# A transformer block with routed experts: the third pair of routed tiles turned from its first rows, and another order of work at the start

## The chip, the cores and the metric

The kernel runs on one core of a Trainium2 chip. The core has five engines that run their own instruction streams: TensorE (PE) multiplies matrices, with a separate record for loading weights (PEld), VectorE (DVE) does elementwise work and small transposes, ScalarE (ACT) activations and copies, GpSimd (POOL) elementwise work and the indirect DMAs, and SyncE (SP) issues most of the other DMAs. The metric is the device time of one execution in microseconds (us); lower is better.

## What is computed

The input is x of 16 sequences, 512 tokens each, 256 numbers a token, all in float32. With xn the layer norm of x over its 256 numbers, the result is

```
out = x + attention(xn) + ffn(xn)

attention:  q = elu(xn Wq + bq) + 1,  k = elu(xn Wk + bk) + 1,  v = xn Wv + bv     (16 heads of 16)
            kv = sum over tokens of k v^T, per head
            out = (q kv) / max(q . sum of k, 1e-6), then Wo and bo

ffn:        shared = swiglu(xn w_in) w_out                                        (hidden 512)
            h = swiglu(xn w1)                                                     (hidden 512)
            one of 2 groups by the larger group logit; in it the best 2 of 4 experts by softmax,
            weighted by their probability times that of the group
            routed = sum over the two experts of weight_e * (h w2_e)
```

## The kernel before, in words

**Sequence by sequence.** The 16 sequences are worked one after another, each as four token tiles of 128. `normalize` (line 249) makes xn on VectorE (bn_stats L263, bn_aggr L265, reciprocal L268, subtract and multiply L270; the square root is ScalarE's, L267) and brings it into the transposed form xnT. For the first two sequences TensorE transposes (L280) and ScalarE copies to SBUF (L283); from the third on xn goes to DRAM, comes back in blocks of 32 rows (`turn`, L232, xb), and one VectorE instruction transposes the blocks (L242). `project` (L304) makes keys and router logits in one product (pk, L312) and queries (pq, L323); VectorE adds the biases (kk L316, lg L317, qq L327) and `feature_map` (L297) applies elu + 1. `route` (L333) computes groups, experts and weights in many small VectorE instructions. `residual` (L289) has POOL add bo to x (L292). These run a sequence ahead as `front` (L725).

**The rest of a sequence.** `summarize` (L464) multiplies xn with the keys, `hidden_rows` (L417) makes h row by row and stores it to a DRAM table h_d (L433), `hidden` (L435) makes the shared hidden part, `mix` (L477) combines the key summary with Wv and Wo, and `gather` (L526) adds shared output and attention for each token tile in PSUM (po, L534, two buffers); VectorE adds it to the residual (L535), and the base row is stored to the same table h_d (L536), behind h.

**The routed tiles.** After the last sequence the tokens are sorted by their pair of experts (`order`, L539). The class `Tiles` (L642) takes two tiles of 128 sorted tokens at a time, 33 such pairs and one single tile. `rows` (L649) fetches their rows of h_d by indirect DMA on POOL's queue, one of each tile (L654), into one of four row buffers which are the old kk, qq, xn and hs. `turn` (L660) transposes h: ScalarE makes 12 copies of quarters (hb, L673) and VectorE 4 + 3 block transposes (L680 straight from the rows, L686 from the copies) into hT, which has two buffers. `sums` (L692) multiplies hT with the two experts' weights side by side (py, L703), VectorE weights both and adds the base (y, L710 and L713), and an indirect DMA on POOL scatters y to the output (L716). With `AHEAD = 3`, the first three pairs are fetched once before the last `gather`, when h is complete but the base isn't, and again after it. Only the first two are turned from the first fetch (L775, L776).

**What sets the order.** [...] `tc.issue_after(ins)` places what is traced inside it behind `ins` on its engine; `tc.keep_in_program_order` keeps an instruction in the program's order. A buffer of a pool is reused when the last reader of its old tile is done. PSUM has six buffers for most products (`ps_mm`) and two for po. At the start, x comes in four pieces on SP's queue, wk and wq on ScalarE's, and the small weights we and wg and the biases on POOL's.

Of the kernel before, what the change touches and what calls it, by code (L numbers as in the profile page):

```python
# [10 lines left out]
FP = mybir.dt.float32  # L11
AF = mybir.ActivationFunctionType
ALU = mybir.AluOpType
AX = mybir.AxisListType

P = 128
# [5 lines left out]
def block_kernel(  # L22
# [29 lines left out]
    nc = tc.nc  # L52
    B, S, D = x.shape
# [7 lines left out]
    NT = S // P  # L61
# [15 lines left out]
    AHEAD = 3  # L77
# [12 lines left out]
    ps_mm = ctx.enter_context(tc.tile_pool(name="ps_mm", bufs=6, space=bass.MemoryType.PSUM))  # L90
# [28 lines left out]
    nc.gpsimd.memset(eps_sb, LN_EPS)  # L119
    ident = const.tile([P, P], FP)  # L120
    make_identity(nc, ident)
    root = const.tile([P, 1], FP)
    nc.scalar.activation(root, eps_sb, AF.Sqrt)

# [5 lines left out]
    nc.gpsimd.dma_start(out=wkr_sb[:, :, D : D + E], in_=we.rearrange("(p c) e -> p c e", p=P))  # L130
    nc.gpsimd.dma_start(out=wkr_sb[:, :, D + E : KR], in_=wg.rearrange("(p c) e -> p c e", p=P))
    wq_sb = wp.tile([P, KD, D], FP)
    nc.scalar.dma_start(out=wq_sb, in_=wq.rearrange("(p c) f -> p c f", p=P))
    bkr_sb = const.tile([P, KR], FP)
    nc.gpsimd.dma_start(out=bkr_sb[:, 0:D], in_=bk.partition_broadcast(P))
    nc.gpsimd.dma_start(out=bkr_sb[:, D : D + E], in_=eb.partition_broadcast(P))
# [4 lines left out]
    for q in range(NQ):  # L141
        nc.gpsimd.dma_start(
            out=bv_sb[ts(q, Q)], in_=bv[ts(q, KD * Q)].rearrange("(c i) -> i c", i=Q)
# [10 lines left out]
    for k in range(KD):  # L154
        for c in range(KD):
            nc.sync.dma_start(
                out=wv_sb[:, k, ts(c, P)].rearrange("p (q i) -> p q i", i=Q), in_=by_quadrant(wv[ts(k, P), :])[:, c]
            )
    wo_sb = wp.tile([P, KD, D], FP)
    for q in range(NQ):  # L160
        nc.sync.dma_start(
            out=wo_sb[ts(q, Q)], in_=wo[ts(q, KD * Q), :].rearrange("(c i) d -> i c d", i=Q)
# [5 lines left out]
    def load_expert(i):  # L168
# [23 lines left out]
        out=before, in_=ones, pattern=[[1, P]],  # L192
# [56 lines left out]
    def normalize(b):  # L249

        xt = xs[b]
        st = small.tile([P, NT, 6], FP, tag="st", name=f"st_{b}")
        mv = small.tile([P, NT, 2], FP, tag="mv", name=f"mv_{b}")
        sd = small.tile([P, NT], FP, tag="sd", name=f"sd_{b}")
        rs = small.tile([P, NT], FP, tag="rs", name=f"rs_{b}")
        xn = xn_all[:, b % 2]

        n = 1 if b == 0 else NT
        made = []
        for g in range(0, NT, n):  # L260
            with tc.issue_after(last_xn[-1].ins) if last_xn else nullcontext():
                for t in range(g, g + n):
                    nc.vector.bn_stats(out=st[:, t, :], in_=xt[:, t, :])  # L263
            for t in range(g, g + n):
                nc.vector.bn_aggr(out=mv[:, t, :], in_=st[:, t, :])  # L265
            with tc.issue_after(last_copy[-1].ins) if last_copy else nullcontext():
                nc.scalar.activation(sd[:, g : g + n], mv[:, g : g + n, 1], AF.Sqrt, bias=eps_sb)  # L267
            nc.vector.reciprocal(rs[:, g : g + n], sd[:, g : g + n])  # L268
            for t in range(g, g + n):
                made.append(nc.vector.tensor_scalar(  # L270
                    xn[:, t, :], xt[:, t, :], mv[:, t, 0:1], rs[:, t : t + 1],
                    ALU.subtract, ALU.mult,
                ))
        last_xn[:] = made[-1:]
        xnT = work.tile([P, KD, S], FP, tag="xnT", name=f"xnT_{b}")
        if b < 2:
            for t in range(NT):
                pt = ps_mm.tile([P, KD, P], FP, tag="mm", name=f"pt_{b}_{t}")
                for c in range(KD):
                    nc.tensor.transpose(  # L280
                        pt[:, c, :], xn[:, t, :].rearrange("p (m c) -> p c m", c=KD)[:, c], ident
                    )
                last_copy.append(nc.scalar.copy(xnT[:, :, ts(t, P)], pt))  # L283
            return xn, xnT, None
        last_copy.clear()
        nc.sync.dma_start(out=xn_d[b % 2].rearrange("(t p) d -> p t d", p=P), in_=xn)
        return xn, xnT, turn(xnT, xn_d[b % 2], "xb", b, "(i c)")
# [13 lines left out]
        nc.scalar.activation(low, low, AF.Exp)  # L301
        nc.vector.scalar_tensor_tensor(y, y, 0.0, low, ALU.max, ALU.add)

    def project(b, xnT):  # L304

        kk = kk_all[:, b % 2]
        qq = qq_all[:, b % 2]
        lg = small.tile([P, NT, E + G], FP, tag="lg", name=f"lg_{b}")
        for t in range(NT):
            pk = ps_mm.tile([P, KR], FP, tag="mm", name=f"pk_{b}_{t}")  # L310
            for k in range(KD):
                nc.tensor.matmul(  # L312
                    pk, lhsT=xnT[:, k, ts(t, P)], rhs=wkr_sb[:, k, :],
                    start=(k == 0), stop=(k == KD - 1),
                )
            nc.vector.tensor_tensor(kk[:, t, :], pk[:, 0:D], bkr_sb[:, 0:D], ALU.add)  # L316
            nc.vector.tensor_tensor(lg[:, t, :], pk[:, D:KR], bkr_sb[:, D:KR], ALU.add)  # L317
        feature_map(b, kk, "km")
        for t2 in range(0, NT, 2):
            pq = ps_mm.tile([P, 2, D], FP, tag="mm", name=f"pq_{b}_{t2}")  # L320
            for t in (0, 1):
                for k in range(KD):
                    nc.tensor.matmul(  # L323
                        pq[:, t, :], lhsT=xnT[:, k, ts(t2 + t, P)], rhs=wq_sb[:, k, :],
                        start=(k == 0), stop=(k == KD - 1),
                    )
            nc.vector.tensor_tensor(  # L327
                qq[:, t2 : t2 + 2, :], pq, bq_sb.unsqueeze(1).to_broadcast([P, 2, D]), ALU.add
            )
        feature_map(b, qq, "qm")  # L330
        return qq, kk, lg
# [191 lines left out]
        qT = one.tile([P, KD, S], FP, tag="qT", name=f"qT_{b}")  # L523
        return qT, turn(qT, q_d[b % 2], "qb", b, "(c i)")

    def gather(b, res, qT, kvo, hs):  # L526

        taken = []
        for t in range(NT):
            po = ps_y.tile([P, D], FP, tag="py", name=f"po_{b}_{t}")  # L530
            parts = [(hs[:, f, ts(t, P)], wout_sb[:, f, :]) for f in range(KH)]
            parts += [(qT[:, c, ts(t, P)], kvo[:, c, :]) for c in range(KD)]
            for i, (a, w) in enumerate(parts):
                nc.tensor.matmul(po, lhsT=a, rhs=w, start=(i == 0), stop=(i == len(parts) - 1))  # L534
            taken.append(nc.vector.tensor_tensor(res[:, t, 0:D], po, res[:, t, 0:D], ALU.add))  # L535
            nc.sync.dma_start(out=h_d[ts(b * NT + t, P), HID:ROW], in_=res[:, t, :])  # L536
        return taken

# [103 lines left out]
    class Tiles:  # L642
# [17 lines left out]
        def turn(self, after=None):  # L660

            n, W = self.n, HID // NQ
            self.hT = work.tile([P, KH, 2 * P], FP, tag="xnT", name=f"hT_{self.tiles[0]}")
            to = self.hT.rearrange("p c (n a j) -> p n c a j", n=2, a=NQ)[:, 0:n]
            near = 1
            there = work.tile([P, NQ - near, 2, W], FP, tag="blocks", name=f"hb_{self.tiles[0]}")  # L670
            for a in range(near, NQ):
                for q in range(NQ):
                    nc.scalar.copy(  # L673
                        there[ts(q, Q), a - near, 0:n, :], self.hg[ts(a, Q), 0:n, ts(q, W)]
                    )
            wait = (lambda: tc.issue_after(after.ins)) if after else nullcontext
            for a in range(near):
                for q in range(NQ):
                    with wait():
                        nc.vector.transpose(  # L680
                            to[ts(q, Q), :, :, a, :],
                            self.hg[ts(a, Q), 0:n, ts(q, W)].rearrange("p n (c i) -> p n c i", i=Q),
                        )
            for a in range(near, NQ):
                with wait():
                    nc.vector.transpose(  # L686
                        to[:, :, :, a, :],
                        there[:, a - near, 0:n, :].rearrange("p n (c i) -> p n c i", i=Q),
                    )
            return self  # L690

        def sums(self):  # L692

            for j, i in enumerate(self.tiles):
                if i % TR == 0:
# [6 lines left out]
                for f in range(KH):  # L702
# [4 lines left out]
                    )  # L707
                base = self.hg[:, j, HID:ROW]
                y = work.tile([P, D], FP, tag="y", name=f"y_{i}", bufs=4)
                nc.vector.scalar_tensor_tensor(  # L710
                    y, py[:, 0, :], base[:, D : D + 1], base[:, 0:D], ALU.mult, ALU.add
                )
                nc.vector.scalar_tensor_tensor(  # L713
                    y, py[:, 1, :], base[:, D + 1 : D + 2], y, ALU.mult, ALU.add
                )
# [6 lines left out]
                tc.declare_no_dep(stored.ins, group="out", reason="no two tiles write to the same row")  # L722
                tc.add_to_no_dep_group("out", stored.ins)

    def front(b, xnT):  # L725

        res = residual(b)
        qq, kk, lg = project(b, xnT)
        route(b, lg, res)
        return res, qq, kk  # L730

    waiting = list(range(G * NL))

    normed = {0: normalize(0)}
    fronts = {0: front(0, normed[0][1])}
    normed[1] = normalize(1)
    queries = {}
    xs[2] = load_x(2)
    for b in range(B):
# [24 lines left out]
            queries[b + 1] = attend(b + 1, fronts[b + 1][1], sums)  # L764
        hs = hidden(b, xnT)
        kvo = mix(b, xk, ksb)
        if b + 2 < B:
            normed[b + 2][2]()
        if b + 1 == B:
            for w in tiles[:AHEAD]:  # L770
                w.rows()
        taken = gather(b, res, qT, kvo, hs)
        if b + 1 == B:

            tiles[0].turn(taken[-2])  # L775
            tiles[1].turn(taken[-1])  # L776

        for e in waiting[: 2 if b + 1 < B else G * NL]:
            load_expert(e)
# [9 lines left out]
    for g, w in enumerate(tiles):  # L789
        if 0 < g < len(tiles) - AHEAD:  # L790
            tiles[g + AHEAD].rows()
        if g + AHEAD - 1 < len(tiles):
            tiles[g + AHEAD - 1].turn()
        w.sums()

    def rest(i):
        if i < TILES:
# [44 lines left out]
```

## Time and profile before

| What | us |
|---|---|
| three runs: lowest, median, highest | 1086.5, 1091.64, 1130.06 |
| the profiled execution: its own time | 1087.99 |
| the profiled execution: span from first to last instruction | 1086.2 |
| TensorE busy, of the span | 1055.5 |
| VectorE, ScalarE, POOL busy | 660.9, 375.9, 243.9 |
| first transpose, first pk on TensorE | 8.18, 10.69 |
| first pk of the second sequence, first phr | 20.13, 31.14 |
| first py of the routed tiles | 833.45 |

The profile names an engine, a line and the tiles that an instruction writes and reads ("py<-w_sb,hT"). A float32 product appears as two records for each matmul, so a routed tile (four matmuls) has eight records of py, a pair sixteen. A wait is written with what ended it, for instance "PE py L703 <- DVE hT L686". PEclk is the share of full speed that TensorE's clock was granted. The few times that TensorE waits are at the start, once after the first sequence, and between the last sequence and the routed tiles.

### The profile page before, as it was taken

Reading aid. Unit: us, or ns where it says so; the run is one execution under the profiler, and the core shown is the slowest. Engines: PE = TensorE matmul, PEld = TensorE weight load, DVE = VectorE, ACT = ScalarE, POOL = GpSimd, SP = SyncE. Lnnn points to the kernel's source line nnn. Section 1 sums busy time; section 2 is a strip of 40 time slices with the busy share of each in tenths; the row PEclk is TensorE's granted clock in tenths of the full one; section 3 lists DMA queues with packets and bytes.
Section 4 is the critical chain, followed back from the end, with each engine's and each line's share of the span. In section 5 each row is a group of like instructions: output and inputs, shape, how many; then the busy total and the mean of one; then the engine's idle time right before and its main releaser. Section 6 shows DMA issues by size and latency. Waiting matters only on the chain.

```text
span 1086.2 us, 11307 instructions
## 1 busy us (share of the span) xinstructions
PE 1055.5 (97%) x3404; PEld 627.5 (58%) x3404; DVE 660.9 (61%) x1744; ACT 375.9 (35%) x703; POOL 243.9 (22%) x313
## 2 busy tenths in 40 slices
PE   6999999999999999999999999999999699999996
PEld 5574747575666657574747575666646244444442
DVE  7947466564647474746556464647395466666663
ACT  3413232223223131313222232212013667777761
POOL 6102011020202020101101020202003555555552
PEclk9999999999999999999999999999999899999999
DMA  7243342433424243423131323221114544555540
GB/s 228 97 117 117 78 135 59 135 92 105 133 69 136 69 136 88 125 59 115 41 116 57 100 72 91 81 63 63 59 40 133 185 136 152 150 151 152 153 151 34
DMA packets 129054, 116.02 MB, mean 107 GB/s; under 512 B 72109, under 2 KB 113597, under 8 KB 128736
## 3 DMA queue, kind: packets, MB, share of 16 engines
q1 hardware_dynamic: 119120, 77.16, 23.7%
q0 software_dynamic: 9456, 37.59, 11.4%
q8 instruction: 29, 0.48, 0.2%
q10 hardware_dynamic: 416, 0.52, 0.1%
q14 instruction: 33, 0.27, 0.1%
HBM read 65.36 MB, written 50.27 MB: 106 GB/s over the span
## 4 chain that ended last, share of the span: by engine, by line
PE 94%; DVE 2%; DMA 1%; issue 1%; ACT 0%; POOL 0%; SPq 0%; POOLq 0%; DVEq 0%; ACTq 0%
PE py L703 21%; PE phr L424 20%; PE phs L443 20%; PE po L534 15%; PE pxk L469 5%; PE pk L312 5%; PE pq L323 5%; PE pm L499 2%; PE pvk L482 1%; PE pks L459 1%; DMA x<-in_x 0%; DMA xn_all<-h_d,source 0%; ACT hb L673 0%; DMA hs_all<-h_d,source 0%; PE pi L614 0%
## 5 line engine op out<-in xcount | busy, mean ns | idle before, releaser
L703 PE MATMUL py<-w_sb,hT 128*128 x536 | 233.5, 599 | 10.0 <-DVE hT L686 10.0
L443 PE MATMUL phs<-xnT,win_sb 128*128 128x512 f32 x512 | 223.6, 593 | 0.0
L424 PE MATMUL phr<-w_sb,xnT 128*128 128x512 f32 x512 | 222.8, 593 | 0.0
L703 PEld LDWEIGHTS py<-w_sb,hT 128*128 128x128 f32 x536 | 103.0, 193 | 140.0 <-issue 138.9
L424 PEld LDWEIGHTS phr<-w_sb,xnT 128*128 128x128 f32 x512 | 97.3, 190 | 114.5 <-issue 106.0
L443 PEld LDWEIGHTS phs<-xnT,win_sb 128*128 128x128 f32 x512 | 97.0, 190 | 113.0 <-issue 110.3
L292 POOL TENSOR_TENSOR res<-x,bo_sb 128x1024 f32<-128x1024 f32 x16 | 37.9, 2369 | 433.9 <-DMA h_d<-res 323.4
L534 PE MATMUL po<-wout_sb,hs_all 128*128 128x256 f32 x512 | 123.6, 380 | 0.0
L535 DVE TENSOR_TENSOR res<-po,res 128x256 f32<-128x256 f32 x64 | 27.2, 424 | 131.8 <-PE po L534 131.8
L534 PEld LDWEIGHTS po<-wout_sb,hs_all 128*128 128x128 f32 x512 | 96.3, 191 | 12.2
L450 DVE TENSOR_TENSOR hs_all<-phs,sa_hs 128x512 f32<-128x512 f32 x64 | 43.5, 680 | 90.7 <-PE phs L443 85.4
L449 ACT ACTIVATE sa_hs<-phs 128x512 f32<-128x512 f32 x64 | 38.2, 597 | 158.4 <-PE phs L443 153.3
L716 POOL DMA_INDIRECT out<-y,goal x67 | 67.6, 1009 | 88.4 <-DVE y L713 78.0
L301 ACT ACTIVATE km<-km 128x1024 f32<-128x1024 f32 x16 | 16.9, 1057 | 177.4 <-DVE km L300 177.4
L432 DVE TENSOR_TENSOR hr<-phr,sa_hr 128x512 f32<-128x512 f32 x64 | 43.8, 684 | 55.7 <-PE phr L424 32.8
L430 ACT ACTIVATE sa_hr<-phr 128x512 f32<-128x512 f32 x64 | 38.0, 597 | 99.2 <-PE phr L424 93.3
L534 PE MATMUL po<-kvo,qT 128*128 128x256 f32 x256 | 67.0, 384 | 0.0
L312 PE MATMUL pk<-wkr_sb,xnT 128*128 128x266 f32 x256 | 61.3, 393 | 2.0 <-DVE xnT L242 1.7
L469 PE MATMUL pxk<-kk_all,xn_all 128*128 128x256 f32 x256 | 58.0, 380 | 0.0
L323 PE MATMUL pq<-wq_sb,xnT 128*128 128x256 f32 x256 | 57.9, 379 | 0.0
L456 POOL TENSOR_TENSOR k<-kk_all 128x512 f32<-128x512 f32 x16 | 27.6, 1727 | 127.8 <-DVE sm L358 125.3
L312 PEld LDWEIGHTS pk<-wkr_sb,xnT 128*128 128x128 f32 x256 | 49.1, 193 | 11.3 <-DVE xnT L242 2.1
(148 smaller groups left out, 1261.5 us busy)
## 6 DMA issues: line engine op xcount, KB each, us to landing
h_d<-hr SPq DMA_DIRECT2D x64, 256.0 KB, 2.6
h_d<-res SPq DMA_DIRECT2D x64, 129.0 KB, 1.9
q_d<-qq_all SPq DMA_DIRECT2D x16, 512.0 KB, 2.8
qb<-q_d SPq DMA_DIRECT2D x64, 128.0 KB, 2.6
w_sb<-in_w SPq DMA_DIRECT2D x64, 128.0 KB, 3.5
x<-in_x SPq DMA_DIRECT2D x15, 512.0 KB, 4.3
xn_d<-xn_all SPq DMA_DIRECT2D x14, 512.0 KB, 3.0
xb<-xn_d SPq DMA_DIRECT2D x56, 128.0 KB, 3.3
```

What stands on the lines that cost most here:

```text
L312: nc.tensor.matmul(pk, lhsT=xnT[:, k, ts(t, P)], rhs=wkr_sb[:, k, :], start=(k == 0), stop=(k == KD - 1),)
L323: nc.tensor.matmul(pq[:, t, :], lhsT=xnT[:, k, ts(t2 + t, P)], rhs=wq_sb[:, k, :], start=(k == 0), stop=(k == KD - 1),)
L424: nc.tensor.matmul(ph, lhsT=xnT[:, k, ts(t, P)], rhs=w1_sb[:, k, ts(half, HID)], start=(k == 0), stop=(k == KD - 1),)
L430: nc.scalar.activation(sa, halves[0], AF.Silu)
L432: nc.vector.tensor_tensor(hr, halves[1], sa, ALU.mult)
L443: nc.tensor.matmul(ph, lhsT=win_sb[:, k, ts(half * KH + f, P)], rhs=xnT[:, k, :], start=(k == 0), stop=(k == KD - 1),)
L449: nc.scalar.activation(sa, halves[0], AF.Silu)
L450: nc.vector.tensor_tensor(h[:, f, :], halves[1], sa, ALU.mult)
L469: nc.tensor.matmul(pxk[:, c, :], lhsT=xn[:, t, ts(c, P)], rhs=kk[:, t, :], start=(t == 0), stop=(t == NT - 1),)
L534: nc.tensor.matmul(po, lhsT=a, rhs=w, start=(i == 0), stop=(i == len(parts) - 1))
L703: nc.tensor.matmul(py.rearrange("p j d -> p (j d)"), lhsT=self.hT[:, f, ts(j, P)], rhs=w2_sb[:, f, bass.ds(regs[i % TR], 2 * D)], start=(f ...
L716: stored = nc.gpsimd.indirect_dma_start(out=out_rows, out_offset=bass.IndirectOffsetOnAxis(ap=self.goal[:, i : i + 1], axis=0), in_=y, in_ ...
```

## The change

The change has three parts.

At the start, TensorE makes eight transposes of the identity into two PSUM tiles that nobody reads, ahead of its first work. The load of wq is issued on SP's queue, behind the four pieces of x, and no longer on ScalarE's. In the first sequence VectorE's bn_stats of a token tile is placed behind the xn of the tile before. TensorE's transposes of the first sequence are made inside `project`, two tiles ahead of the two pk that use them, and TensorE's transposes keep the program's order.

In `gather`, the third and fourth addition of VectorE (L535) are placed behind the block transpose of xnT of the sequence after next (L242), where there is one.

For the routed tiles, the third pair too is turned from its first fetch, behind the last addition of the last `gather`, and no longer after the second fetch in the loop over the pairs. The first pair's y is placed behind the third pair's last transpose on VectorE.

```diff
     make_identity(nc, ident)
+    for i in range(2):
+        idle = ps_mm.tile([P, P], FP, tag="mm", name=f"idle_{i}")
+        for _ in range(4):
+            nc.tensor.transpose(idle, ident, ident)
...
-    nc.scalar.dma_start(out=wq_sb, in_=wq.rearrange("(p c) f -> p c f", p=P))
+    nc.sync.dma_start(out=wq_sb, in_=wq.rearrange("(p c) f -> p c f", p=P))
...
-        last_xn[:] = made[-1:]
+            last_xn[:] = made[-1:]
         xnT = work.tile([P, KD, S], FP, tag="xnT", name=f"xnT_{b}")
         if b < 2:
-            for t in range(NT):
+            def place(t):
                 pt = ps_mm.tile([P, KD, P], FP, tag="mm", name=f"pt_{b}_{t}")
                 for c in range(KD):
-                    nc.tensor.transpose(
+                    tc.keep_in_program_order(nc.tensor.transpose(
                         pt[:, c, :], xn[:, t, :].rearrange("p (m c) -> p c m", c=KD)[:, c], ident
-                    )
+                    ))
                 last_copy.append(nc.scalar.copy(xnT[:, :, ts(t, P)], pt))
+
+            if b == 0:
+                return xn, xnT, place
+            for t in range(NT):
+                place(t)
             return xn, xnT, None
...
-    def project(b, xnT):
+    def project(b, xnT, place=None):
...
         for t in range(NT):
+            if place and t % 2 == 0:
+                place(t)
+                place(t + 1)
             pk = ps_mm.tile([P, KR], FP, tag="mm", name=f"pk_{b}_{t}")
...
-    def gather(b, res, qT, kvo, hs):
+    def gather(b, res, qT, kvo, hs, placed):
...
-            taken.append(nc.vector.tensor_tensor(res[:, t, 0:D], po, res[:, t, 0:D], ALU.add))
+            with tc.issue_after(placed.ins) if placed and t > 1 else nullcontext():
+                taken.append(nc.vector.tensor_tensor(res[:, t, 0:D], po, res[:, t, 0:D], ALU.add))
...
-                    nc.vector.transpose(
+                    self.turned = nc.vector.transpose(
                         to[:, :, :, a, :],
...
-        def sums(self):
+        def sums(self, after=None):
...
-                nc.vector.scalar_tensor_tensor(
-                    y, py[:, 0, :], base[:, D : D + 1], base[:, 0:D], ALU.mult, ALU.add
-                )
+                with tc.issue_after(after.ins) if after else nullcontext():
+                    nc.vector.scalar_tensor_tensor(
+                        y, py[:, 0, :], base[:, D : D + 1], base[:, 0:D], ALU.mult, ALU.add
+                    )
...
-    def front(b, xnT):
+    def front(b, xnT, place=None):
...
-    fronts = {0: front(0, normed[0][1])}
+    fronts = {0: front(0, *normed[0][1:])}
...
-        if b + 2 < B:
-            normed[b + 2][2]()
+        placed = normed[b + 2][2]() if b + 2 < B else None
...
             tiles[0].turn(taken[-2])
-            tiles[1].turn(taken[-1])
+            for w in tiles[1:AHEAD]:
+                w.turn(taken[-1])
...
-        if g + AHEAD - 1 < len(tiles):
+        if 0 < g < len(tiles) - AHEAD + 1:
             tiles[g + AHEAD - 1].turn()
-        w.sums()
+
+        w.sums(tiles[AHEAD - 1].turned if g == 0 else None)
```

More of the change, by code (lines that the diff above doesn't have):

```diff
@@ L723, in sums @@
                 tc.add_to_no_dep_group("out", stored.ins)
-    def front(b, xnT):
+    def front(b, xnT, place=None):
         res = residual(b)
-        qq, kk, lg = project(b, xnT)
+        qq, kk, lg = project(b, xnT, place)
         route(b, lg, res)
@@ L771, in block_kernel @@
                 w.rows()
-        taken = gather(b, res, qT, kvo, hs)
+        taken = gather(b, res, qT, kvo, hs, placed)
         if b + 1 == B:
             tiles[0].turn(taken[-2])
-            tiles[1].turn(taken[-1])
+            for w in tiles[1:AHEAD]:
+                w.turn(taken[-1])
         for e in waiting[: 2 if b + 1 < B else G * NL]:
```

## The prediction

> **What bounds the kernel now.** I read the page's busy times first, then TensorE's own waits, then the timeline around each wait. The page's first two parts:
>
> ```profile
> PE 1055.5 (97%) x3404; PEld 627.5 (58%) x3404; DVE 660.9 (61%) x1744; ACT 375.9 (35%) x703; POOL 243.9 (22%) x313
> ...
> PE   6999999999999999999999999999999699999996
> ...
> PEclk9999999999999999999999999999999899999999
> ```
>
> TensorE is busy 97% of the span, and three slices of 40 are not full: the first, slice 32 and the last. No part of the diff touches the matmuls, so only idle or slow-clocked TensorE time can be won. TensorE's waits, all of them (engine, line, what released it: total us, times, longest):
>
> ```profile
> PE py L703 <- DVE hT L686: 10.0, 2, 9.2
> PE pt L280 <- DVE xn_all L270: 8.5, 2, 8.2
> PE pk L312 <- DVE xnT L242: 1.7, 1, 1.7
> PE pk L312 <- DVE qq_all L327: 0.3, 1, 0.3
> ```
>
> Each is a part of the change: the start (8.5 and 0.3), one wait after the first sequence (1.7), and the seam from the last sequence to the routed tiles (10.0, of it 9.24 at once). The timeline of the seam, start and duration in us (PE, then the queues that lead to it):
>
> ```profile
> 833.45 14.00 PE L703 MATMUL py<-w_sb,hT 128*128 x32 [0.75 <-DVE hT L686]
> 856.69 13.89 PE L703 MATMUL py<-w_sb,hT 128*128 x25 [9.24 <-DVE hT L686]
> ...
> 845.96 0.95 POOL L654 DMA_INDIRECT xn_all<-h_d,source  x1 [0.30 <-issue]
> 850.77 1.78 DVE L680 STREAM_TRANSPOSE hT<-xn_all 32x256 f32<-32x256 f32 x4 [2.82 <-DMA xn_all<-h_d,source]
> 851.10 4.97 ACT L673 COPY hb<-xn_all 32x256 f32<-32x256 f32 x12 [13.76 <-DMA xn_all<-h_d,source]
> ```
>
> TensorE does 32 records (two pairs of tiles) and stops. The third pair's rows were fetched twice; the second fetch is last of eight in POOL's queue (845.96), and the pair is transposed only from that one: ScalarE sat idle 13.76 us for it, copied for 4.97, and VectorE's transposes followed. The clock pays too (windows; the last three columns are PEclk, DMA share, GB/s):
>
> ```profile
> 847.00:850.00 3.00, 0.45 (x2) 0.00 (x0) 0.91 (x2) 0.00 (x0) 2.17 (x3) 1.00 0.87 300
> 853.00:856.00 3.00, 0.00 (x0) 0.00 (x0) 2.77 (x7) 2.90 (x8) 1.43 (x2) 0.50 0.78 197
> 859.00:862.00 3.00, 3.00 (x5) 1.06 (x4) 0.89 (x2) 2.89 (x8) 0.49 (x1) 0.50 0.51 142
> 862.00:865.00 3.00, 3.00 (x8) 1.40 (x7) 0.97 (x2) 2.90 (x8) 0.40 (x1) 0.90 0.00 0
> ```
>
> [...] 9.24 us idle, then 0.50 until about 862.6, weight loads 0.86 us apart there against 0.43 before. [...] wq's issue took 0.55 us on ScalarE. [...] here a 128x8 operation of two inputs (L352) took 2.35 us under res on POOL (L292, 16.94 to 21.7), against 0.15 elsewhere.
>
> **The change, part by part.** (1) *Third pair from its first rows.* Its first fetch is issued at 826.48 and 827.74; by the first pair's (issued to 822.67, copies from 827.37: 4.7 us) it lands near 832.5. ScalarE ends the second pair's copies at 837.33, so the third's 12 run to 842.3. There are two hT buffers; the third pair takes the first pair's, free when its 16 records end: 833.45 + 16 x 0.429 = 840.3. VectorE is idle from 837.8 to 844.4, which covers four L680 (1.78) and three L686 (3 x 0.45): ready at about 843.5, 3.7 us before TensorE wants it at 847.2. The idle 9.24 goes, and the slow clock: 856.69 to 862.57 at half speed cost 2.94. Together 12.2. The 0.75 ahead of the first pair stays, since its transposes are not moved.
>
> What is late next? The first pair's y operations now stand behind the third pair's transposes on VectorE (who waits: POOL's scatters, and the fetch of pair five into the same rows). But they waited for the second fetch until 844.42 anyway, after 843.5, so that order costs nothing. The second fetch of pair three must wait until its rows are read (842.3); its turn on POOL comes at 844.70: nothing either. Pair four (rows issued by 838.41, ScalarE free at 842.3) is copied by about 848 and transposed from 847.2 to 850.4, wanted at 854.1. Pair five is the tight one: fetch issued at 849.85 and 851.14, landing 4.0 to 4.8 later (872.15 to 876.12 in the routed stage; 845.96 to 850.77), 4.97 of copies, one last transpose of 0.45: 860.6 to 861.5, wanted at 833.45 + 4 x 6.87 = 860.9. So a new stall of 0 to 0.6; later pairs gain on it, because each POOL round of four indirect DMAs takes 5.2 of the 6.87 us. I take 0.5, at most 1.5. Part (1): -11.7.
>
> (2) *VectorE in the gather: xnT ahead of the third and fourth additions.* After the first sequence:
>
> ```profile
> 71.56 0.43 DVE L535 TENSOR_TENSOR res<-po,res 128x256 f32<-128x256 f32 x1 [2.17 <-PE po L534]
> 71.91 1.24 DVE L242 STREAM_TRANSPOSE xnT<-xb 128x1024 f32<-128x1024 f32 x1
> ```
>
> Its blocks landed at about 61 (last issue 57.7, 3.3 to landing), and VectorE idles 1.67 us ahead of the second addition: the 1.24 fits in, and TensorE's 1.67 goes. The two additions now wait behind it, and TensorE's po behind them through two PSUM buffers; with blocks there 8 us early that is nothing. Later (113.78, 721.67) the transpose already stands first. -1.6.
>
> (3) *The start.* (a) xn per tile: VectorE now finishes t0 by 4.7 and t1 by 6.4, where before t0's reciprocal waited to 7.44 behind the third bn_stats (its x landed at 7.10). Each later tile takes the whole chain (8.35 to 10.13: 1.78), so the last xn ends between 9.7 and 10.6 against 10.13: no gain for sure. (b) wq moves from ScalarE's queue to SP's, behind the four x pieces: it may bring x up to 1 us earlier, and puts x1 and every weight behind it on SP 0.55 later; x1 was not waited for at 10.05, w1 is wanted only at 31, and the DMA engines are empty from 26 to 32. (c) pk by halves: pk can begin when wg is there, 2.67 + 6.3 = 9.0, against 10.69; but pt of t2 and t3 now follows pk of t1 on TensorE, with a copy to wait for (0.4). (d) Eight idle transposes, 16 records at 0.21 cold: 2.8 to 6.2, under time in which TensorE idled anyway. If the clock is warm by 9: pk 1.8, pt 1.0, copy 0.4, pk 1.8 ends at 14.1; if it stays cold to 12.65 as before: 3.5 + 1.0 + 0.4 + 1.8 ends at 15.7; before, 15.4. So +1.3 to -0.3 on TensorE. But TensorE's next pk wait is for VectorE's qq (L327, 19.31), held by the 2.35 us under POOL's res, which starts when bo lands (16.94); eb and gb land at 12.5 and 13.1, and lg additions put early would hold VectorE for them up to 2 us. The start therefore lies between 1.5 gained and 1.5 lost; I take -0.2.
>
> Sum, against the profiled execution: span 1086.2 - 11.7 - 1.6 - 0.2 = 1072.7, and 1.8 around it (1087.99 - 1086.2) gives 1074.5. The three runs have 1086.5 as lowest, 1091.64 as median: the profiled one is near their low end, so I say **1075.0**.
>
> **Rivals.** *The stall moves* (0.15): something in the ring is later than I have it, say copies or y operations in another order on VectorE, so that pair five waits for 3 to 6 us[...]: 1079 to 1083. For it: pair five's margin is nil. Against: TensorE does not wait once after 856.69 while the same ring runs. *No effect at the seam* (0.05): the third pair's transposes stay behind the second fetch, because the buffers' order holds them: 1086.2 - 1.8 + 1.8 = about 1086. Against: VectorE's idle time and the freed buffer both precede it. *Slower* (0.03): the new wait in the gather. If xb's blocks landed later than TensorE's third po, TensorE would stall there in each of 14 sequences. They land about 9 us ahead of the third addition (721.67 against 730.77); from 10 us later on, each us costs 14, and beyond 11 the gain of 13.5 is gone: about 1090 to 1100. *Best case* (in the forecast's own tail): all of 9.24 + 2.94, the 1.67 and 1.5 at the start: 1088.0 - 15.4 = 1072.6, or about 1070 with a run as low as the lowest.
>
> **Numbers.** The forecast (0.77) spans 1070 to 1079; the moved stall reaches 1083; that is the range. A change of 2%, about what a measurement of this kernel can tell from no change, would need 1069.8 or less against the median: 0.06, since the idle time open to the change gives at most 1.5%. Slower by over 2%: 0.03. Within: 0.91.
>
> **What would show it.** The wait of py for hT falls from 10.0 to about 1 with no second wait over 1 us; PEclk keeps 9 in slice 32; L680 of the third pair starts near its predecessor's end on TensorE, not after a DMA; the wait of pk for xnT is gone; L242 of the first sequence stands before the third L535; the first pk stands near 9. I am wrong if ScalarE waits for xn_all at the seam, if pair five waits over 1 us, or if the first long phr starts more than 1.5 us away from 31.1.

## The result

The changed kernel takes **1077.49 us** (median of six, 1076.5 to 1079.89) against 1089.85 of the kernel before measured beside it (1085.69 to 1130.06): a ratio of 0.9901, 95% interval 0.9876 to 0.9925. The ratio is one of means and leaves out the execution of 1130.06 as a slow one, 3.5% above the highest of the other five (1085.69 to 1091.64). The profiled execution took 1077.43, its span is 1075.7. Measured again later, the same program gave 1083.03 (1080.07 to 1083.66) against 1087.49, a ratio of 0.9949 (0.9931 to 0.9968). The gain is therefore a half to one per cent by the two ratios, 0.3 to 1.2 by their intervals, and the difference between the two rounds is itself a finding (below, the seam).

The page after, busy times and slices:

```profile
PE 1056.1 (98%) x3412; PEld 627.5 (58%) x3412; DVE 662.6 (62%) x1744; ACT 376.1 (35%) x703; POOL 244.4 (23%) x313
...
PE   7999999999999999999999999999999999999996
...
PEclk9999999999999999999999999999999999999998
```

Slice 32 is full now and its clock is back at 9. TensorE's waits after (engine, line, releaser: total us, times, longest):

```profile
PE pk L324 <- ACT xnT L287: 4.1, 2, 2.1
PE idle L125 <- POOL ident masks.py:199: 2.8, 1, 2.8
PE py L716 <- DVE hT L699: 1.5, 2, 0.8
PE pt L284 <- DVE xn_all L274: 0.8, 1, 0.8
```

The 9.2 for hT and the 1.7 for xnT of the third sequence are gone. New is a pair of waits of pk for ScalarE's copies, both at the start. Cut at TensorE's milestones, the span of the two profiled executions differs as follows:

| Stretch | before | after | difference |
|---|---|---|---|
| to the first phr | 31.14 | 33.72 | +2.58 |
| to the third sequence's first pk | 42.05 | 40.23 | -1.82 |
| to the first py | 760.26 | 760.14 | -0.12 |
| first py to last py | 242.11 | 230.71 | -11.40 |
| last py to the end | 10.66 | 10.91 | +0.25 |
| span | 1086.22 | 1075.71 | -10.51 |

The seam in the timeline after (start, duration, idle before in brackets):

```profile
834.09 27.73 PE L716 MATMUL py<-w_sb,hT 128*128 x64 [0.74 <-DVE hT L699]
862.58 17.83 PE L716 MATMUL py<-w_sb,hT 128*128 x41 [0.76 <-DVE hT L699]
...
838.02 4.98 ACT L686 COPY hb<-xn_all 32x256 f32<-32x256 f32 x12
856.99 4.97 ACT L686 COPY hb<-kk_all 32x256 f32<-32x256 f32 x12 [7.57 <-DMA kk_all<-h_d,source]
...
852.45 0.98 POOL L667 DMA_INDIRECT kk_all<-h_d,source  x1 [0.30 <-issue]
```

TensorE now runs 64 records, four pairs, and first waits at pair five, 0.76 us. ScalarE copies the third pair (xn_all) with no wait for a DMA. Pair five's rows (kk_all) are the next late thing: issued to 852.45 behind everything in POOL's queue, and copied from 856.99, 4.5 us later. In two of the windows that were at half clock before (last three columns PEclk, DMA share, GB/s):

```profile
853.00:856.00 3.00, 3.00 (x8) 1.33 (x7) 0.85 (x2) 0.00 (x0) 2.39 (x3) 1.00 0.74 230
859.00:862.00 3.00, 2.83 (x7) 0.95 (x5) 0.72 (x3) 2.88 (x9) 1.94 (x2) 1.00 0.64 186
```

Eight records in 3 us in place of none, at 1.00 in place of 0.50.

The start in the timeline after:

```profile
8.28 0.30 ACT L271 ACTIVATE sd<-mv,eps_sb 128x1 f32<-128x1 f32 x1 [1.23 <-DVE mv L269]
8.48 0.62 ACT L287 COPY xnT<-pt 128x256 f32<-128x256 f32 x2
13.26 0.80 ACT L287 COPY xnT<-pt 128x256 f32<-128x256 f32 x2 [4.16 <-PE pt L284]
13.95 0.30 ACT L271 ACTIVATE sd<-mv,eps_sb 128x4 f32<-128x4 f32 x1
...
17.45 2.30 DVE L274 TENSOR_SCALAR xn_all<-x,mv,rs 128x256 f32<-128x256 f32 x1
20.27 1.75 DVE L361 TENSOR_TENSOR ex<-lg,mx 128x32 f32<-128x32 f32 x1
...
22.14 0.24 ACT L368 ACTIVATE ex<-ex 128x40 f32<-128x40 f32 x1 [3.68 <-DVE ex L364]
22.28 1.18 ACT L287 COPY xnT<-pt 128x256 f32<-128x256 f32 x4
...
16.88 5.10 POOL L301 TENSOR_TENSOR res<-x,bo_sb 128x1024 f32<-128x1024 f32 x2 [3.63 <-DMA bo_sb<-in_bo]
...
22.69 3.86 PE L324 MATMUL pk<-wkr_sb,xnT 128*128 128x266 f32 x16 [2.10 <-ACT xnT L287]
```

ScalarE works in the order of issue: the copies of the first two pt, the first of them transposed by 5.4, stand behind all four square roots, so pk starts at 8.88 although wg had landed at 7.07. The other two pt follow two slow pk, their copies come at 13.26, and the square root of the second sequence waits behind them until 13.95 (11.76 before). So VectorE's last xn of the second sequence and its ex (the router's logits less their maximum) fall under POOL's res, which begins when bo lands, and take 2.30 and 1.75 us in place of 0.40 and 0.19 (before, at 14.53 and 16.93). ScalarE's exponential of ex waits for them until 22.14, its copies of the second sequence's pt stand behind that, and the second sequence's pk behind the copies, at 22.69 (20.13 before). The first phr comes 2.58 later than before.

### The profile page after: what moved, and what is told of

Its sections match the earlier page's. It is cut to its first block, busy times and chain, and to the rows that moved or that the text cites. A ratio compares the mean times of both kernels' runs of the same rounds, so it can differ in the third digit from the quotient of the medians.

```text
span 1075.7 us, 11323 instructions
## 1 busy us (share of the span) xinstructions
PE 1056.1 (98%) x3412; PEld 627.5 (58%) x3412; DVE 662.6 (62%) x1744; ACT 376.1 (35%) x703; POOL 244.4 (23%) x313
## 4 chain that ended last, share of the span: by engine, by line
PE 94%; DVE 2%; DMA 1%; issue 1%; POOL 0%; ACT 0%; POOLq 0%; DVEq 0%
PE phr L436 20%; PE phs L455 20%; PE py L716 20%; PE po L546 15%; PE pk L324 6%; PE pxk L481 5%; PE pq L335 5%; PE pm L511 2%; PE pvk L494 1%; PE pks L471 1%; DMA xn_all<-h_d,source 0%; DMA kk_all<-h_d,source 0%; DVE xn_all L274 0%; DMA qq_all<-h_d,source 0%; PE pi L627 0%
## 5 line engine op out<-in xcount | busy, mean ns | idle before, releaser
L716 PE MATMUL py<-w_sb,hT 128*128 x536 | 230.5, 592 | 1.5 <-DVE hT L699 1.5
```

The costliest lines, as they stand in the source:

```text
L716: nc.tensor.matmul(py.rearrange("p j d -> p (j d)"), lhsT=self.hT[:, f, ts(j, P)], rhs=w2_sb[:, f, bass.ds(regs[i % TR], 2 * D)], start=(f ...
```

## The experiments

Two theories were at stake. At the **start**: the halves put work behind work in in-order queues and VectorE's small operations under POOL's res, against the rivals that a single late square root does it, or that the cold clock does. At the **seam**: what holds pair five, its fetch in POOL's queue or something else. The time of the profiled execution, and first phr, first py and pair five's wait in its trace:

| Run | time, us | first phr | first py | pair five's wait |
|---|---|---|---|---|
| changed kernel | 1077.43 | 33.72 | 834.09 | 0.76 |
| e1, start as before | 1080.53 | 29.16 | 830.32 | 5.91 |
| e2, start alone | 1091.89 | 35.34 | 837.67 | (pair three 9.39) |
| e3, seam alone | 1083.77 | 29.65 | 832.38 | 5.84 |
| e4, square root ahead of two copies | 1083.36 | 36.46 | 836.85 | 2.25 |
| e5, changed kernel again | 1080.07 | 33.81 | 834.21 | 3.54 |
| e6, e1 again | 1079.41 | 29.52 | 830.71 | 3.37 |
| e7, all four pt first | 1079.23 | 30.30 | 831.34 | 3.82 |
| e8, 24 transposes | 1080.98 | 35.13 | 836.63 | 1.88 |
| e9, 12 matmuls | 1081.56 | 34.90 | 836.83 | 2.26 |
| e10, e1 without second fetch | 1072.60 | 29.65 | 830.84 | none |
| e11, e1 with short second fetch | 1077.04 | 32.70 | 832.80 | 1.65 |
| e12, e11 with 24 transposes | 1079.95 | 33.47 | 833.75 | 2.09 |

The kernel before, beside these: 1090.83 for e1 to e4 (one run), 1087.49 for e5 to e7, 1088.0 for e8 to e10 (one run), 1087.43 for e11 and e12.

### One part at a time (e1, e2, e3)

e1 is the changed kernel with its start as before; e2 the kernel before with the changed start only; e3 the kernel before with the seam only. In e1 the transposes of the first sequence are also back in their old loop (left out here); e3 takes back the last piece, in `gather`, too:

```diff
-    for i in range(2):
-        idle = ps_mm.tile([P, P], FP, tag="mm", name=f"idle_{i}")
-        for _ in range(4):
-            nc.tensor.transpose(idle, ident, ident)
...
-    nc.sync.dma_start(out=wq_sb, ...)
+    nc.scalar.dma_start(out=wq_sb, ...)
...
-            last_xn[:] = made[-1:]
+        last_xn[:] = made[-1:]
...
-            if place and t % 2 == 0:
-                place(t)
-                place(t + 1)
...
-            with tc.issue_after(placed.ins) if placed and t > 1 else nullcontext():
-                taken.append(nc.vector.tensor_tensor(...))
+            taken.append(nc.vector.tensor_tensor(...))
```

> The start as before, the gather and the routed tiles as in the change. Theory (the start lost 2.6 us, the rest kept all that it gained): the first pk of the second sequence is back near 20.1, the first phr near 31.1, the first py near 831.6 and the span near 1073.1. Rival (the missing 3 us went in the seam or the gather, and the late start is made up by slack later): the span stays at 1075.7 or more although phr starts at 31.1.

> The kernel before with the new start alone. Theory: pk of the second sequence near 22.7 and the first phr near 33.7 as in the changed kernel, the seam's 9.24 wait and the 1.67 wait for xnT unchanged, span 1086.2 + 2.6 = 1088.8. Rival (the late start costs nothing by itself): span 1086.2.

> The kernel before with the third pair turned from its first rows, and nothing else. Theory: the first phr at 31.1, the wait of pk for xnT stays at 1.67, first py at 833.45, no wait at the third pair, 0.76 at the fifth; span 1086.2 - 9.24 - 2.94 + 0.76 = 1074.8. Rival (the seam gives back more than the 0.76 later on): 1077 or more.

Only what was expected of e2 came out in kind; e1 and e3 have spans of 1078.8 and 1082.1, where 1073.1 and 1074.8 were expected. In e2 the start alone is 4.2 us late at the first phr and not early, and its time is no better than the kernel before. e1 and e3 have the first phr 4.1 to 4.6 earlier than the changed kernel, and 1.5 to 2.0 earlier than the kernel before, whose start they share; why is read below. e3 keeps the 1.67 wait after the first sequence, e1 doesn't: that part is the gather's. But e1 gives back at pair five what its start wins, 5.91 us of wait and then 6.83 us of half clock.

### The start (e4, e7)

e4 places the second sequence's square root behind ScalarE's second copy, not its fourth; e7 keeps everything but the halves.

```diff
-            with tc.issue_after(last_copy[-1].ins) if last_copy else nullcontext():
+            with tc.issue_after(last_copy[1 if b == 1 else -1].ins) if last_copy else nullcontext():
...
-            if place and t % 2 == 0:
-                place(t)
-                place(t + 1)
+            if place and t == 0:
+                for u in range(NT):
+                    place(u)
```

> The changed kernel, but the square root of the second sequence stands behind ScalarE's second copy of xnT and no longer behind its fourth. Theory (the late square root, 13.95, makes xn of the second sequence late, so that its last tile falls under POOL's res): the square root near 12.4, the last xn near 15, pk of the second sequence near 20.3, the first phr near 31.3. Rival (the slow clock of the first pk and POOL's res at 16.9 hold VectorE anyway): phr stays near 33.7.

> The changed kernel, but all four token tiles of the first sequence are transposed ahead of its first pk; warm-up, wq's queue and VectorE's order tile by tile stay. Theory (the halves put two transposes and two copies, and behind them the second sequence's square root, after two slow pk): the square root near 12.5, pk of the second sequence near 20.5, first phr near 31.5. Rival (VectorE's order or wq's queue is to blame): phr at 33.5 or later, as in the changed kernel.

e4 missed, its first phr at 36.46, 2.7 later still, and it is no test of the late square root. VectorE waited there for the second sequence's x until 12.54 (10.64 in the changed kernel), so the square root came at 14.25, no sooner than the 13.95 of the changed kernel, and the two copies now waited behind it, to 14.46. A better test lies in e8 and e9 below: they have the square root at 12.49 and 12.55, and yet their first phr is at 35.13 and 34.90. So an early square root alone doesn't mend the start. e7 holds: with all four pt ahead of the first pk, pk starts later (9.81) but pq sooner (14.96 against 16.02) and the first phr is at 30.30. That speaks for the halves; how much of it is theirs is weighed below.

How the start loses is read from all thirteen new traces and that of before. Where both ex begin before res does, they cost little; e6, VectorE and POOL:

```profile
16.28 0.19 DVE L349 TENSOR_TENSOR ex<-lg,mx 128x32 f32<-128x32 f32 x1
16.39 0.16 DVE L352 TENSOR_TENSOR ex<-lg,mx 128x8 f32<-128x8 f32 x1
...
17.13 5.67 POOL L292 TENSOR_TENSOR res<-x,bo_sb 128x1024 f32<-128x1024 f32 x2 [4.05 <-DMA bo_sb<-in_bo]
```

This is so in e1, e3, e6, e7 and e10, and these five have the first phr between 29.16 and 30.30. In the other nine at least one xn or ex of VectorE lies under res, for 1.6 to 2.5 us each, and the first phr is between 31.14 (before, one operation caught) and 36.46. The start of before has ex at 15.8 to 17.0 and res between 16.2 and 17.2, and wins in four of six traces; the changed start and its variants with the halves, with ex at 17.4 to 20.3, lose in all six. e7 has ex at 16.93 and won because bo landed late (17.68); against the 16.88 of the changed kernel it would have been caught, so only 1.1 us of its 3.4 (pq) is sure to be its own. Not every operation of VectorE is stretched: in the changed kernel, under the same res, ex (two inputs) took 1.75 and xn (`tensor_scalar`) 2.30, but the two reductions just ahead of that xn (17.29, under res already) 0.18 and 0.15, as in e6 ahead of res. That moving res would cure it was not tried.

### The warm-up (e8, e9)

The changed kernel with 24 idle transposes, and with 12 float32 matmuls of the identity in their place:

```diff
-        for _ in range(4):
+        for _ in range(12):
             nc.tensor.transpose(idle, ident, ident)
```

```diff
-        for _ in range(4):
-            nc.tensor.transpose(idle, ident, ident)
+        for _ in range(6):
+            nc.tensor.matmul(idle, lhsT=ident, rhs=ident, start=True, stop=True)
```

> The changed kernel with 24 idle transposes instead of 8 (records of 0.246 us, so 2.8 to about 8.7 us, up to the first pk). If transposes do not count as busy for the clock: the first pk's records stay 0.43 us apart, the clock is full only near 14.6 us, and the first long phr stays near 33.7. If they do count, the last idle transposes run at 0.12 us, the first pk's records are 0.22 apart from 8.9 on, and the first phr comes 1.5 to 3 us earlier.

> The changed kernel with 12 idle float32 matmuls of the identity by itself (two records each, some 24 records of 0.2 us) in place of the 8 idle transposes. Both theories of the transposes expect the clock full by about 7 us here, pk records 0.22 apart from the first, and the first phr 1.5 to 3 us earlier than 33.7, unless ScalarE's and VectorE's queues, not the clock, set the second sequence's start; then phr stays within 1 us of 33.7.

TensorE in e8:

```profile
2.81 4.27 PE L125 MATMUL idle<-ident 128*128 128x128 f32 x24 [2.81 <-POOL ident masks.py:199]
22.39 5.57 PE L324 MATMUL pk<-wkr_sb,xnT 128*128 128x266 f32 x16 [2.29 <-ACT xnT L287]
```

The clock was full from 5.8 us with transposes and from 6.2 with matmuls, and the two pk of each half took 2.06 in both, not 3.91 and 2.50. In e8 only transposes had run by 5.8, and there they quicken from one every 0.21 us to one every 0.11. So in this run transposes alone brought the clock to full; the changed kernel's eight, 1.97 us long, had left it cold until 14.6. It brought nothing: the first phr is 1.2 to 1.4 later than in the changed kernel, where 1.5 to 3 sooner was expected if the clock set the start. In e8 pq starts at 13.8, 2.2 sooner, but the second sequence's pk still waits for ScalarE's copies behind ex, to 22.39, and after that wait of 2.29 us the clock was at half again for 3.41 us. The clock was not what set the start.

### The seam (e5, e6, e10, e11, e12)

e5 is the changed kernel unedited and e6 is e1 unedited, both timed.

> The changed kernel once more, in the same rounds as the next one. Theory (the stall of 2 to 6 us at the fifth pair, seen with the three kernels run last, belongs to how that execution went and not to their edits): pair five waits between 0.7 and 6 us here too, and the time is 1077 to 1082, against 0.99 of the kernel before. Rival (the changed kernel's own start keeps the seam free of it): 0.8 us at pair five again and 1077.

> The changed kernel with the start as before, in the same rounds. Theory (the new start costs 2.6 to 4.5 us and nothing gives it back): 2.5 to 4.5 us below the changed kernel in the medians, first phr 2.6 to 4.5 us earlier. Rival (an earlier arrival at the seam is lost again at pair five): the same time as the changed kernel, within 1 us, and a longer stall at pair five.

The medians are 1083.03 and 1082.12, ratios 0.9949 and 0.994 (0.9916 to 0.9963): a first phr 4.3 us earlier is worth 0.9 in the medians, which the intervals don't tell from nothing, where 2.5 to 4.5 was expected. The profiled executions show where the rest went. e6 has its first py 3.5 earlier and waits as long at pair five (3.37 against 3.54), but its wait is followed by 6.83 us of half clock, which costs 3.4, and e5's by none. The timeline of e5:

```profile
834.21 27.73 PE L716 MATMUL py<-w_sb,hT 128*128 x64 [0.74 <-DVE hT L699]
865.49 7.11 PE L716 MATMUL py<-w_sb,hT 128*128 x16 [3.54 <-DVE hT L699]
...
857.64 4.97 ACT L686 COPY hb<-kk_all 32x256 f32<-32x256 f32 x12 [8.04 <-DMA kk_all<-h_d,source]
...
861.52 0.48 DVE L724 SCALAR_TENSOR_TENSOR y<-py,xn_all 128x256 f32<-128x256 f32 x1 [8.34 <-remote]
```

ScalarE had pair five's rows at 857.64, only 0.5 us later in the ring than in the first profile, and yet its wait is 3.54. VectorE stood still for 8.34 us ahead of the y of pair three, whose first tile TensorE had ended at 851.64. In the record of semaphores, TensorE's updates for that tile and the next two came in one burst at 861.49 to 861.68, 9.8 us late for the first, and the y began 0.03 us after it; pair five's transposes, behind the y on VectorE, came late with them. The same burst is in e1, e3, e4 and e6 to e9, 8 to 10 us late for its first tile; in the traces of the kernel before, of the changed kernel's first profile and of e11 and e12 every update came within 0.02 us of its tile's end.

These four traces differ from the ten others in one thing more: their record of updates is whole, sixteen for every DMA (8416 of 8416 for the first two, 9440 of 9440 for e11 and e12). In the ten others 8 to 11% of the DMAs' updates and 52 to 65 of VectorE's some 1380 are missing. The eight with the burst are all among these ten. That VectorE stood still is no gap in the record, but what makes the signals late may be what makes records go missing, and belong to how these executions ran or were traced, or to the chip, rather than to the kernel.

So pair five has two things against it. One is the chain through POOL's queue: eight fetches and two scatters of 1.25 to 1.34 us each, back to back, then the landing, then 4.97 of copies. The other is TensorE's late signal. Both were put to the test by taking the second fetch away (e10), or two thirds of its bytes (e11, the gather storing its rows into a second table as well), both with the start as before; e12 is e11 with 24 idle transposes.

```diff
-    for w in tiles[:AHEAD]:
-        w.rows()
```

```diff
             nc.sync.dma_start(out=h_d[ts(b * NT + t, P), HID:ROW], in_=res[:, t, :])
+            nc.sync.dma_start(out=base_d[ts(b * NT + t, P), :], in_=res[:, t, :])
...
+                nc.gpsimd.indirect_dma_start(
+                    out=self.hg[:, j, HID:ROW], out_offset=None, in_=base_d,
+                    in_offset=bass.IndirectOffsetOnAxis(ap=self.source[:, i : i + 1], axis=0),
+                )
...
     for w in tiles[:AHEAD]:
-        w.rows()
+        w.bases()
```

> The changed kernel with its start as before, and without the second fetch of the first three pairs' rows (left out: their last additions are those of the first fetch, so rows of the last sequence in these pairs lack a part). It takes six whole-row fetches out of the seam. If the late signals of TensorE that hold pair five's transposes come from the load on the DMA engines: VectorE's first transpose of pair five starts within 1 us of the end of pair three's matmuls, pair five waits under 0.8 us (3.4 and 5.9 with the fetches), the clock keeps full speed, and the span is 3 to 6 us under 1078. If the load has no part in it, pair five still waits 2 to 6 us.

> The changed kernel with its start as before, and with the second fetch of the first three pairs taken from a table of the additions alone (258 of a row's 770 numbers; the gather stores them there as well): as many fetches and rows at the seam, a third of the bytes. If the bytes at the seam hold TensorE's signals: pair five waits under 1 us, the span is 1071 to 1074, the median 1073 to 1076. If it is the number of fetches and rows, or their place in POOL's queue: pair five still waits 2 to 6 us and the median is 1079 to 1083, as with whole rows (1082.1).

> The previous kernel with 24 idle transposes ahead, and nothing else of the changed start. They end near 7.1 us, where the first pt can begin. With the clock full from about 6 us on, pk of the first sequence takes 3.7 instead of 4.5 us and pt 0.3 to 0.7 less: 0.5 to 1.5 us off the first phr (29.5) and off the time, if VectorE's normalization does not set pk(1) instead; then nothing, within 0.3 us.

e10, TensorE, POOL and ScalarE:

```profile
830.84 49.62 PE L704 MATMUL py<-w_sb,hT 128*128 x115 [0.75 <-DVE hT L687]
...
846.29 0.98 POOL L655 DMA_INDIRECT kk_all<-h_d,source  x1 [0.30 <-issue]
...
851.10 4.97 ACT L674 COPY hb<-kk_all 32x256 f32<-32x256 f32 x12 [5.39 <-DMA kk_all<-h_d,source]
```

115 records without a wait, the rows copied from 20.3 us after the first py (22.9 in the changed kernel), and 1072.60: the gain of the seam and that of an early first phr are both kept once pair five doesn't wait. The late signals are gone with the wait: VectorE read the tile that ended at 848.28 at 848.60, and the one late update that the record shows (856.70, for a tile ended at 855.14) held nothing up. So e10 shortens POOL's queue and loses the late signals at once, and doesn't tell which of the two counts. It also leaves work out: this is a bound and not a version. e11 missed: its profiled execution has all signals in time, but pair five waits 1.65, its rows copied from 856.59:

```profile
862.19 18.26 PE L714 MATMUL py<-w_sb,hT 128*128 x42 [1.65 <-DVE hT L697]
```

That is POOL's queue, as long as with whole rows; with 2.09 in e12 it is what remains when no signal is late. That the fewer bytes brought the signals in time isn't shown: e11 and e12 ran on another chip (4) than the eight with the burst (0, 5 and 9). Its median is 1080.54 (1073.76 to 1081.71), ratio 0.9921 (0.9892 to 0.9949), not told apart from e6. Of e11's six executions two with a mean clock of 0.997 took 1073.8 and 1077.0, three with 0.994 took 1081.3 to 1081.7, and one lies between (0.996, 1079.8). In e1, e3 and e6 0.994 goes with 6.83 us of half clock after pair five; whether those three had it, and late signals with it, was not seen. e12 (1080.12; ratio 0.9929, 0.9907 to 0.9951) shows no gain from the warm-up, where 0.5 to 1.5 us or nothing was expected: its first pk, four tiles, took 3.76 us against 5.62 in e11, but ex was caught again (2.35), VectorE then waited 4.03 for an x that had been placed ahead of the queries' bias, and the first phr came at 33.47.

What makes TensorE's signals late stays open. In all eight traces that have it, the burst came 1.6 to 2.7 us after POOL had ended a back-to-back run of indirect DMAs, which speaks for POOL's DMAs as the cause (though POOL stops because the y is missing that the signals hold up); against it, the changed kernel's first profile, e11 and e12 have the same run of them and no late signal.

## Why the prediction was right, and where it was not

The time held: 1075.0 was forecast and 1077.49 measured, in the range; and within 2% of before. Some of that is luck: in the later round the same program's median was 1083.03, at the very end of the range, and its first profile has the shortest wait at pair five of all traces with this seam and its second fetch. By its steps:

**Step (1), the third pair: right.** Its transposes ended at 844.2, 0.7 later than the forecast 843.5, of which 0.64 is the later first py. The 9.24 and the half clock went. Forecast -11.7; measured -11.40 between first and last py. Of its term for pair five, "0.5, at most 1.5", the first profile shows 0.76; pair five's fetch, "issued at 849.85 and 851.14" in that sum, was issued at 851.16 and 852.45. But **the bound was wrong**: in the ten other traces with this seam and its second fetch the wait is 1.65 to 5.91, and 1.65 and 2.09 even where every signal is in time. "The stall moves", at 1079 to 1083, is about what the seven executions of e5 did (1080.07 to 1083.66). Its counter-argument failed: that TensorE never waited after 856.69 in the kernel before proved no slack in the ring, since the 9.24 us stall had itself given pair five that time. The late signals were in no step of it, and the trace of the kernel before has none.

**Step (2), the gather: right.** The 1.67 us wait is gone (1.6 forecast), the stretch that holds it is 1.82 shorter, and no new wait of po appeared in it.

**Step (3), the start: mis-sized, and past its own bound.** Forecast -0.2, "between 1.5 gained and 1.5 lost"; measured +2.58, and the first phr is more than the 1.5 us from 31.1 that the prediction named as its own refutation. pk did begin at 9 (8.88), but each later term of TensorE's sum lay at its cold end (clock full at 14.6, not 9), and pq began at 16.02 where 15.7 was the latest. The larger part is the term for res: one operation of 2.35 was put in, as before; the later order put two under it, 2.30 and 1.75. That the second sequence's square root went behind copies that the halves delay is a part of it, but e8 and e9 show that it isn't all. And the 2.35 is no fixed cost: of the five other traces with the start as before four have no ex under res and one has two. The eight idle transposes are eight records, not sixteen: 2.81 to 4.78, not to 6.2.

**Rivals.** No effect at the seam, and slower through the gather: neither. The sum of the misses, +2.8 at the start and +0.3 at the seam, is the 3.0 between the forecast span of 1072.7 and 1075.7.

## What to carry to other kernels

When a stall is taken away, ask what slack it gave to the items behind it: a ring that runs without waits after a stall may do so because of the stall. Work put ahead on one in-order queue moves what stands behind it on that queue (here ScalarE's square root of the second sequence, from 11.76 to 13.95); follow each displaced instruction to the engine it releases, and see which time-sensitive neighbour (here POOL's res, under which ex took 1.75 us and not 0.19) it then meets. Time a gain of a few microseconds in more than one round before calling its size known.

## What had not been expected of the hardware

In eight of the traces TensorE's semaphore updates arrived in a burst 8 to 10 us after the end of the first of their tiles, while TensorE itself ran on; nothing but a wait on another engine shows it. All eight are traces with a part of their update records missing, and no whole one has it, so that this belongs to every execution isn't shown. A wait of TensorE's as short as 2.09 us (e12, ended at 863.57) was followed by 3.41 us of half clock, one of 3.54 (e5) by none: every spell of half clock between the start and the last matmuls was 3.41, 6.83 or 10.24 us long (3.41 in e12, 6.83 in e1, e3 and e6, 10.24 in the kernel before, 852.33 to 862.57), whole multiples of 3.41. Laid on the grid of 3.41 us that each trace's clock changes keep to (from full speed at the start to the next half clock it is 839.68 us in the trace of before, 246 steps of 3.413, and 1054.72 in that of the changed kernel, 309 steps), the 2.09 of e12 and the 2.25 of e4, which half clock followed, fall within one step, while the 2.26 of e9, which none followed, is cut into 1.80 and 0.46 and the 3.54 of e5 into 1.96 and 1.58. So in these traces what a short wait cost went with where it fell on that grid. And 24 float32 transposes brought the clock to full by 5.8 us (e8), 24 records of matmuls by 6.2 (e9).
